# Two batch rows interleaved at the start of an attention and feed-forward kernel, an expansion ahead of the last scores, and the bias on another engine

## The chip, the core and the metric

One core of a Trainium2 chip runs the program. Its engines are TensorE (PE; its weight loads are listed apart as PEld), VectorE (DVE), ScalarE (ACT), GpSimd (POOL) and SyncE (SP, which here only issues transfers). Each engine takes its instructions in a fixed order and waits where one is not ready. The metric is the time of one execution on the device in microseconds (us); less is better.

## What is computed

```python
x = L0_attn_x                                # 8 rows of 512 tokens, 256 wide
x = x + _L0_attn_ref(_layernorm(x), gamma, w_qkv, w_out)
x = x + _L0_ffn_ref(_layernorm(x), router_w, w1, b1, w2, b2)

# attention: 16 heads of 64
xn = rms_norm(x, gamma);  q, k, v = split(xn @ w_qkv)
out = softmax(q * scale @ k.T) @ v;  return out @ w_out
# feed-forward: 8 experts' router, the best two, one shared expert
expert_out = gelu(xt @ w1 + b1) @ w2 + b2
return expert_out * sum(combine)             # sum of the best two's normalized shares
```

The inputs and outputs are float32. `b2` enters each token scaled by that token's share, as all of `expert_out` does.

## The kernel before, in words

**Precision.** Every matmul of size is done in float16 in three parts: a value is split into a high half (rounded) and a low half (what is left), and high x high, low x high and high x low are summed (`PARTS`, L515). So each operand costs a rounding (the "high" function, on ACT or DVE) and a subtraction (the "low" function, on DVE). Weights are scaled by a power of two that is found on the device: sums of squares (`squares`, `square_v`, L206, `square_wo`, L397), a small matmul with ones (`total`, L217), and then nine to twelve tiny DVE instructions (`find_qk`, `find_v`, `find_o`, `find_w`, L265 to L302). After that the weight is split (`split_wv` L383, `split_qk1` L378, `split_wo` L407).

**Attention.** A pair is two heads of one row; a row has 8 pairs, and there are 8 rows. For a pair, `project_qk` (L546) makes Q and K into a ring of two buffers, `scores` (L575) makes four tiles of 128 queries by 512 keys for both heads, of which it returns the row maxima (`top`, DVE), the exponentials (`exp`, ACT, 4 of 128x512 for two tiles), the rounding to `hl` (`high`, ACT) and the low half (`low`, POOL) followed by a transposing transfer into `hT` on SP. `weigh` (L619) multiplies with V six tiles (`LAG`, three steps) later, `divide` (L639) divides by the row sums on DVE, `transpose_o` (L651) turns the result, `project` (L670) applies `w_out` for half of the heads and adds to x. `make_v` (L517) makes V for eight heads of 128 tokens. Row statistics and normalization of the next row are `sums1` (DVE), `scale1`, `scale1_last` and `normalize` (POOL), `transpose_rows` (PE) or, from row 3 on, `split_rows` with a transposing transfer.

**Order.** The order is written out by hand. The main loop (L1072) takes one step `d` per two score tiles, ND = 128 steps. Work beside it is entered with `at(step, pos, fn, ...)` (L853); `pos` says where in the step it runs: "d" after the maxima (one step later than named), "a" matmul groups after the scores, "e" after the exponentials on ACT, "b" after the weighing, "z" at the end.

```python
for d in range(ND + LAG // 2 + 1):
    steps = [scores(n) for n in (2 * d, 2 * d + 1)] if d < ND else []
    for top, _, _, _ in steps: top()
    take_lows(); run(d, "d"); groups = run(d, "a")
    for _, exp, _, _ in steps: exp()
    run(d, "e"); take_highs(groups); take_lows()
    for _, _, high, low in steps: high(); low()
    w = 2 * d - LAG
    if 0 <= w < NS: weigh(w); weigh(w + 1); divide(w // 2)
    take_highs(run(d, "b")); run(d, "z")
```

PSUM holds two score tiles (`ps`), one `po` for the weighing, and a ring of three banks (`bank`, L354) for all other groups, so the group that is third after another waits until that one's result was read.

Before the loop, the first weights are loaded, row 0 is normalized and transposed, and q0, k0 (the weights of heads 0 to 7) are split. In the first steps of the loop come v0 and v1, then q1 and k1 (heads 8 to 15), then `w_out`. Rows are taken one after the other, all 8 pairs of row 0 first. Tuples at L34 say which early roundings are done on DVE.

**Feed-forward.** After the last scores, `expand` (L991) makes h = gelu(y w1 + b1) for one of 8 pieces of 128 columns (6 matmuls, one Gelu on ACT, a rounding on ACT, a low half on DVE), `contract` (L1026) multiplies 8 pieces with w2 for 128 tokens (24 matmuls) and adds bias and x with two DVE instructions and a transfer out. Expansions of a row alternate with contractions of the row before it (L1128). The first six pieces (`EARLY`) of the first row run in the last three steps, between the last weighings.

Of the kernel before, what the change touches and what calls it, by code (L numbers as in the profile page):

```python
# [26 lines left out]
P = 128  # L27
# [4 lines left out]


VECTOR_QK, VECTOR_V, VECTOR_O = (5, 8, 11, 12, 13, 18), (0, 1), (3,)  # L34
CAST_BOTH = (21,)
EARLY = 6
# [46 lines left out]
def preln_block(  # L83
# [71 lines left out]
    for name, off, eng in (  # L155
        ("q0", 0, nc.scalar), ("k0", INNER, nc.sync), ("v0", 2 * INNER, nc.sync),
        ("v1", 2 * INNER + 512, nc.sync),
    ):
        t = staged(f"w_{name}", wqkv_r[:, :, off : off + 512], eng)
        raw[name] = [t[:, c, :] for c in range(NC)]  # L160
    w_r = small.tile([P, NC, NE], F32, name="w_r")
# [35 lines left out]
    def square(name, col, src, scale=1.0):  # L197

        pool, what = (hl_p, "hT") if name in ("qk0", "v", "qk1") else (stage, "stage")
        junk = pool.tile([P, 1024], BF16, tag=what, name="junk", bufs=HTB if what == "hT" else SB)  # L200
        nc.scalar.activation(
            junk[:, 0 : src.shape[-1]], src, AF.Square, scale=scale,
            accum_out=sums[name][:, col[0], col[1] : col[1] + 1],
        )

    def square_v(name, col, src, scale=1.0):  # L206
        pool, what, n = (hl_p, "hT", HTB) if name in ("v", "qk1") else (stage, "stage", SB)
        junk = pool.tile([P, 512], BF16, tag=what, name="junk", bufs=n)
        nc.vector.scalar_tensor_tensor(
            junk, src, scale, src, ALU.mult, ALU.mult,  # L210
            accum_out=sums[name][:, col[0], col[1] : col[1] + 1],
        )

    def new_sums(name, k, m):
        sums[name] = stat.tile([P, k, m], F32, name=f"sums_{name}")

    def total(name):  # L217

        _, k, m = sums[name].shape
        pn = bank("pn")  # L220
        nc.tensor.matmul(
            pn[:, 0 : k * m], ones, sums[name].rearrange("p k m -> p (k m)"), start=True, stop=True
        )
        return pn[:, 0 : k * m].rearrange("p (k m) -> p k m", m=m), [
            pn[:, 128 * i : 128 * i + k] for i in range(1, 4)
        ]
# [30 lines left out]
    def with_gamma(*key):  # L257

        f = stat.tile([P, 2, NC], F32, name="f_" + "".join(map(str, key)))
        s = powers_of[key if len(key) > 1 else key[0]]  # L260
        factors[key if len(key) > 1 else key[0]] = f
        for i in range(2):
            nc.scalar.activation(f[:, i, :], gam1, AF.Copy, scale=s[:, i : i + 1])
# [24 lines left out]
    def find_v(n2):  # L288
        added(n2)
        s, u, z = powers("v", n2)  # L290
        powers_of["v"] = s
        factors["1/v"] = inverses("v", u, z)

    def find_o(n2):
        added(n2)
        factors["o"], u, z = powers("o", n2)
        si = inverses("o", u, z)
        f = stat.tile([P, 2], F32, name="f_o")
        nc.vector.tensor_tensor(f, si[:, 0:2], factors["1/v"], ALU.mult)
        factors["1/ov"], factors["1/r"] = f, si[:, 2:3]  # L300
# [21 lines left out]
    with ExitStack() as att:  # L322
# [17 lines left out]
        for b in range(1, XB):  # L340
            load_x(b)
# [3 lines left out]
        xnT, O, OT, po, hT = {}, {}, {}, {}, {}  # L345
        made = {}
# [36 lines left out]
        def split_wv(c, j, eng):  # L383
            if "v" not in factors:
                with_gamma("v")
            cols = ts(j, 512)
            f = factors["v"][:, j, c : c + 1]
# [129 lines left out]
        def make_v(b, t, j):  # L517
# [4 lines left out]
            assert b == 0 or made.get(("pv", b - 1), 0) >= 16 * (j + 1)  # L522
            k = 0
            for i, m in PARTS:
                for c in range(NC):
# [5 lines left out]
            vt = VT[t][:, 8 * j : 8 * j + 8, :]  # L531
# [3 lines left out]
                    nc.vector.tensor_copy if b == 0 and 4 * j + t in VECTOR_V  # L535
# [10 lines left out]
        def project_qk(pair, n):  # L546
# [11 lines left out]
            dst = QK[pair % RING][n]  # L558
            hi, lo = dst[:, 0, :], dst[:, 1, :]

            def high():
                f = factors["out", p // (NP // 2)][:, n : n + 1]
                if 2 * pair + n in VECTOR_QK:
# [11 lines left out]
        def scores(n):  # L575
# [3 lines left out]
            pair, t = divmod(n, NT)  # L579
            need(2, "qk", pair)  # L580
            q, k = QK[pair % RING]
# [19 lines left out]
            def high():  # L601
                if n in CAST_BOTH:
# [16 lines left out]
        def weigh(n):  # L619

            pair, t = divmod(n, NT)
            b, p = divmod(pair, NP)
            need(NT, "v", b, p // 4)
            done("pv", b)
# [3 lines left out]
            for h in range(2):  # L628
                for c in range(NT):
                    v = VT[c][:, 2 * p + h, :]  # L630
# [8 lines left out]
        def divide(k):  # L639
            pair, t = k // 2, k % 2 * 2  # L640
# [10 lines left out]
        def transpose_o(pair):  # L651
# [3 lines left out]
            for t in range(NT):  # L655
# [5 lines left out]
                    nc.vector.tensor_copy if pair in VECTOR_O  # L661
# [138 lines left out]
        for name, k, m in (("qk0", 2, NC), ("v", 2, NC), ("qk1", 2, NC), ("o", 3, 2), ("w", 3, 4)):  # L800
# [10 lines left out]
        for c in range(NC):  # L811
            square_v("v", (0, c), raw["v0"][c], gam2[:, c : c + 1])
# [20 lines left out]
        squares("v", 1, "v1")  # L833
        squares("qk1", 0, "q1", [0])
# [6 lines left out]
        def start_v():  # L841
            find_v(total("v"))
# [53 lines left out]
        at(3, "d", split_wv, 0, 1, nc.scalar)  # L896
        at(2, "d", split_wv, 1, 1, nc.scalar)
        at(4, "e", split_qk1, "q", 0, nc.vector)
        at(4, "e", split_qk1, "q", 1, nc.scalar)
        at(5, "e", split_qk1, "k", 0, nc.vector)  # L900
        at(5, "e", split_qk1, "k", 1, nc.vector)
        at(-1, "d", squares, "qk1", 0, "q1", [1])
        at(0, "z", squares, "qk1", 1, "k1", [0])
        at(2, "b", squares, "qk1", 1, "k1", [1])
        at(3, "b", find_rest, find_qk, 1, "qk1")
        at(2, "d", load_small)
        at(3, "d", load_wo, 0)
        at(5, "d", square_wo, 0, 0)
        at(8, "d", square_wo, 0, 1)
        at(3, "d", load_wo, 1)  # L910
        at(6, "d", square_wo, 1, 0)
        at(6, "d", square_wo_v, 1, 1)
        at(4, "d", square_wr)
        at(10, "b", find, find_o, "o")
        at(12, "d", split_wr)
        at(11, "d", split_wo, 0, nc.scalar)
        at(12, "e", split_wo, 1, nc.scalar)
        at(12, "d", split_wo, 2, nc.scalar)
        at(16, "d", split_wo, 3, nc.scalar)
        for n in (1, 2):  # L920
            for j in range(2):
# [5 lines left out]
                for i in range(2):  # L927
                    at((46, 50, 54, 58, 62, 66, 70, 74)[4 * (n - 1) + 2 * j + i], "z", split_w, n, j, i)
        at(35, "e", square_b1)
        at(44, "b", find, find_w, "w")  # L930
        for b in range(B):
            s0 = 16 * b
            for p in range(NP):
                at(s0 + 2 * p - 2, "a", project_qk, b * NP + p, 0)
                at(s0 + 2 * p - 2, "a", project_qk, b * NP + p, 1)
                if (b, p) != (B - 1, NP - 1):
                    at((s0 + 2 * p + 1 + LAG // 2 + 1) if b else (5, 7, 11, 11, 14, 15, 17, 19)[p], "b", transpose_o, b * NP + p)
            for t in range(NT):
                at(s0 + (13 + 2 * t if b else (13, 15, 17, 19)[t]), "a", project, b, 0, t)
                at(s0 + 3 + 2 * t if b else (5, 8, 4, 10)[t], "a", make_v, b, t, 1)  # L940
                at((s0 - 5 + 2 * t if b > 1 else (11, 13, 13, 17)[t]) if b else (1, 1, 1, 2)[t], "a", make_v, b, t, 0)
            if b + 1 < B:
                at(s0 - 5 if b else 5, "d", scale1_rest, b + 1)
                at(s0 - 4 if b else 5, "d", scale1_last, b + 1)
                for t in range(NT):
                    at(s0 + 21 + 2 * t, "a", project, b, 1, t)
                    at(s0 - 9 + t // 2 if b else (1, 1, 2, 1)[t], "d", sums1, b + 1, t)
                    at(s0 + (1 + t if b else (5, 6, 6, 6)[t]), "d", normalize, norm1, b + 1, t, "x")
                at(s0 - 6 if b else 3, "d", scale1, b + 1)
                if b + XB < B:  # L950
                    for t in range(NT):
                        at(s0 + 30 + 2 * t, "d", load_x_piece, b + XB, t)
                if b + 1 < XD:
                    for c in range(NC):
                        at(s0 + (6 + 2 * c if b else (8, 9)[c]), "b", transpose_rows, b + 1, c)
                else:
                    for k in range(4):
                        at(s0 + (4, 6, 6, 7)[k], "zd"[k // 2], split_rows, "x", b + 1, k)
# [32 lines left out]
        def expand(j, f):  # L991
# [12 lines left out]
            ph = ps_s.tile([P, 2, S], F32, tag="ps", name="ph")[:, 0, :]  # L1004
# [11 lines left out]
            def gelu():  # L1016
# [3 lines left out]
                nc.scalar.activation(hi, h, AF.Copy, scale=factors["h"])  # L1020

            return gelu, lambda: nc.vector.scalar_tensor_tensor(
                lo, h, factors["h"], hi, ALU.mult, ALU.subtract
            )

        def contract(j, t):  # L1026
# [5 lines left out]
            for f in range(NF):  # L1032
# [8 lines left out]
                r, pf[:, :D], factors["1/hw2"], b_2, ALU.mult, ALU.add  # L1041
            )
            nc.vector.scalar_tensor_tensor(
                r, r, comb[:, b, t : t + 1], x2[b][:, t, :], ALU.mult, ALU.add
# [12 lines left out]
        for f in range(EARLY):  # L1057
            at(ND + f // 2, "a", expand, 0, f)
# [13 lines left out]
        for d in range(ND + LAG // 2 + 1):  # L1072
# [10 lines left out]
            take_lows()  # L1083
# [21 lines left out]
        for j in range(1, B):  # L1105
# [7 lines left out]
            if j + 3 < B and order[j + 3] < B - XB:  # L1113
                put(j, 11, load_x2, order[j + 3])
            put(j, 0, both, router_logits, b)
            for k in range(12):
                put(j, min(k + 1, 11), route_step, b, k)
        nc.scalar.activation(first, ones[:, 0:1], AF.Gelu_apprx_tanh)
# [51 lines left out]
```

## Time and profile before

| what | value |
|---|---|
| time, median of 3 runs | 959.67 us (959.57 to 960.41) |
| the profiled execution: time, span | 960.66 us, 958.9 us |
| PE matmul | busy 933.7 us (97%), 11244 matmuls |
| ACT | busy 838.8 us (87%) |
| DVE | busy 733.2 us (76%) |
| POOL | busy 702.6 us (73%) |
| granted TensorE clock, mean | 0.997 |
| start of the first scores, PE | 19.83 us |
| first Gelu, ACT | 774.50 us |
| last matmul group to the end | 954.9 to 958.9 us |

Each engine's timeline gives the start and the length of its instructions and, in brackets, how long the engine was idle ahead of one and what ended that. Instructions of one kind that follow each other stand in one line (x2, x12), whose length is that of the whole group. All instructions of the kernel body carry the line of the helper that issues them (L54); the operation and the tiles tell them apart: `ps` scores, `mx` maxima, `e` exponentials, `hl` the halves of e, `po` weighing, `pot` transposed result, `pqk`, `pv`, `pp`, `ph`, `pf` the groups of Q and K, V, `w_out`, expansion and contraction.

### The profile page before, as it was taken

To read this page: it belongs to the slowest core of one execution; us is meant where nothing else is said; L and a number is where in the kernel's file an instruction comes from. 1 tells how busy PE (TensorE), PEld (TensorE's weight loads), DVE (VectorE), ACT (ScalarE), POOL (GpSimd) and SP (SyncE) were. 2 spreads that over 40 slices of the span, in tenths; PEclk is the share of its full clock that TensorE was granted. 3 is DMA by queue.
4 is the path that set the end of the run, shared out by engine and by line. 5 is a ranking of instruction groups with operands and counts; after the bars stand their busy time and mean duration, and the time that the engine had idled before them with its cause. 6 is when DMAs were issued, how large, how long until landed. Compare 5 with 4: busy or idle time off the path is not lost.

```text
span 958.9 us, 27882 instructions
## 1 busy us (share of the span) xinstructions
PE 933.7 (97%) x11244; PEld 598.5 (62%) x11244; DVE 733.2 (76%) x1325; ACT 838.8 (87%) x1275; POOL 702.6 (73%) x717
## 2 busy tenths in 40 slices
PE   8789999999999999999999999999999999999998
PEld 5345566666666666666666666666666667666666
DVE  6999888888788878788877777777877756655553
ACT  5988899899999999999999999999999986677772
POOL 1688788798888888988888888887888953434400
PEclk9999999999999999999999999999999999999999
DMA  6599899999999999999999999999999971222211
GB/s 220 117 201 191 165 209 204 214 202 198 194 221 202 202 214 209 219 205 207 195 213 184 198 191 185 189 194 193 186 184 197 185 150 34 72 84 77 52 43 39
DMA packets 580624, 163.96 MB, mean 171 GB/s; under 512 B 562960, under 2 KB 578448, under 8 KB 580496
## 3 DMA queue, kind: packets, MB, share of 16 engines
q1 hardware_dynamic: 579952, 161.40, 84.5%
q8 instruction: 88, 1.44, 0.6%
q10 hardware_dynamic: 544, 0.79, 0.2%
q14 instruction: 40, 0.33, 0.1%
HBM read 14.82 MB, written 6.29 MB: 22 GB/s over the span
## 4 chain that ended last, share of the span: by engine, by line
DVE 33%; ACT 27%; PE 26%; issue 7%; POOL 4%; DMA 2%; ACTq 0%; POOLq 0%; DVEq 0%
ACT e L54 19%; DVE mx L54 13%; PE pf L54 9%; PE ph L54 8%; DVE QT L54 4%; DVE O L54 4%; DVE VT L54 4%; DVE KT L54 4%; POOL hl L54 3%; ACT QT L54 3%; PE po L54 2%; ACT VT L54 2%; PE pp L54 2%; PE ps L54 2%; PE pqk L54 2%
## 5 line engine op out<-in xcount | busy, mean ns | idle before, releaser
L54 POOL TENSOR_TENSOR hl<-e,hl 128x512 f16<-128x512 f32 x512 | 585.7, 1176 | 120.4 <-issue 78.5
L54 ACT ACTIVATE e<-ps,mx 128x512 f32<-128x512 f32 x512 | 310.4, 691 | 47.1 <-DVE mx L54 39.1
L54 DVE TENSOR_REDUCE mx<-ps 128x2 f32<-128x1024 f32 x256 | 300.2, 1213 | 1.9 <-PE ps L54 1.9
L54 ACT CAST hl<-e 128x1024 f16<-128x1024 f32 x256 | 258.8, 1081 | 0.0
L54 PEld LDWEIGHTS <-hT 128*128 128x128 f16 x6144 | 203.6, 97 | 33.3 <-issue 5.3
L54 PE MATMUL po<-VT,hT 128*128 128x65 f16 (+1 forms) x6144 | 207.8, 193 | 2.6 <-DVE O L54 1.2
L54 PE MATMUL ps<-KT,QT 64*128 64x512 f16 x1536 | 190.5, 378 | 8.1 <-ACT e L54 6.6
L54 PEld LDWEIGHTS <-wqk 128*128 128x128 f16 x768 | 69.9, 98 | 105.4 <-issue 27.2
L54 PEld LDWEIGHTS <-QT 64*128 64x128 f16 x1536 | 66.3, 94 | 85.0 <-issue 19.8
L54 PE MATMUL pqk<-xT,wqk 128*128 128x512 f16 x480 | 110.7, 380 | 0.4 <-ACT lg L54 0.4
L54 DVE SCALAR_TENSOR_TENSOR QT<-pqk,ab,QT 128x512 f16<-128x512 f32 x64 | 48.0, 750 | 71.8 <-ACT QT L54 71.7
L54 DVE SCALAR_TENSOR_TENSOR h<-h,s_w,h 128x512 f16<-128x512 f32 x64 | 50.0, 783 | 64.8 <-ACT h L54 64.7
L54 PE MATMUL pp<-wo,OT 128*128 128x256 f16 x768 | 94.9, 273 | 0.0
L54 PEld LDWEIGHTS <-OT 128*128 128x128 f16 x768 | 70.2, 98 | 32.6 <-issue 15.3
L54 PE MATMUL ph<-yT,w1s 128*128 128x512 f16 x384 | 89.5, 379 | 0.1
L54 PE MATMUL pf<-w2s,h 128*128 128x256 f16 x768 | 88.4, 273 | 0.0
L54 ACT ACTIVATE h<-ph,b,si_w 128x512 f32<-128x512 f32 x64 | 49.3, 770 | 41.0 <-PE ph L54 40.9
L54 PEld LDWEIGHTS <-h 128*128 128x128 f16 x768 | 75.2, 98 | 14.4
L54 DVE TENSOR_TENSOR VT<-pv,VT 128x512 f16<-128x512 f32 x64 | 43.8, 689 | 50.1 <-ACT VT L54 49.9
L54 PE MATMUL pqk<-xnT,wqk 128*128 128x512 f16 x288 | 66.9, 380 | 1.9 <-DVE OT L54 1.4
L54 PEld LDWEIGHTS <-w1s 128*128 128x128 f16 x384 | 37.0, 98 | 36.8 <-issue 0.3
L54 PE MATMUL pv<-wv,xT 128*128 128x512 f16 x240 | 58.3, 379 | 0.0
(147 smaller groups left out, 929.9 us busy)
## 6 DMA issues: line engine op xcount, KB each, us to landing
hT<-hl SPq DMA_TRANSPOSE x256, 4.0
w<-in_L_ffn_w_dram SPq DMA_DIRECT2D x32, 128.0 KB, 2.8
out_dram<-res SPq DMA_DIRECT2D x32, 128.0 KB, 1.7
x<-x SPq DMA_DIRECT2D x16, 128.0 KB, 2.6
x<-in_L_attn_x_dram SPq DMA_DIRECT2D x16, 128.0 KB, 2.7
x2s<-x SPq DMA_DIRECT2D x4, 512.0 KB, 3.6
x<-in_L_attn_x_dram SPq DMA_DIRECT2D x3, 512.0 KB, 7.5
w_v<-in_L_attn_w_qkv_dram SPq DMA_DIRECT2D x2, 512.0 KB, 8.2
```

Source lines behind the costliest of these rows:

```text
L54: i = method(*args, **kw)
```

## The change

1. **Interleaving.** The order of the work is by groups (row, half of the heads): (0,0), (1,0), (0,1), (1,1), and from row 2 on as before. So q1, k1 and v1 are needed only from group 2 on (step 16; their Q and K are made from step 14, V from step 11), while row 1 must be normalized and transposed by step 3. x of row 1 is loaded ahead of v1. V's buffers are addressed by the parity of the group.
2. **Moves that go with it.** The squares, searches and splits of v1, q1, k1 and w_out stand in other steps and partly on other engines; v0 and v1 get a search each. For row 1 `scale1_last` now stands ahead of `scale1_rest`: the multiplication is done before the reciprocal is taken. Which roundings DVE does is listed by place in the new order.
3. **Last scores.** `EARLY` is 7. The first piece is expanded in step ND-2 into a bank of the ring instead of a score buffer; its Gelu is held until step ND. For the first row the rounding of h moves from ACT to DVE. From step ND on the low halves are no longer taken ahead of the weighing but in the next step.
4. **Bias.** `add_bias` on POOL adds share x b2 to x ahead of the contraction, so that one DVE instruction is left behind each contraction in place of two.

Cut to its core:

```diff
-VECTOR_QK, VECTOR_V, VECTOR_O = (5, 8, 11, 12, 13, 18), (0, 1), (3,)
-CAST_BOTH = (21,)
-EARLY = 6
+EARLY = 7
...
-        ("v1", 2 * INNER + 512, nc.sync),
...
+    load_x(1)
+    t = staged("w_v1", wqkv_r[:, :, 2 * INNER + 512 : 3 * INNER], nc.sync)
...
-    def find_v(n2):
+    def find_v(j, n2):
         added(n2)
-        s, u, z = powers("v", n2)
+        s, u, z = powers(f"v{j}", n2)
...
+        groups = [(0, 0), (1, 0), (0, 1), (1, 1)] + [(b, j) for b in range(2, B) for j in range(2)]
+        turn = {g: u for u, g in enumerate(groups)}
+        seq = [b * NP + j * NP // 2 + p for b, j in groups for p in range(NP // 2)]
...
-        squares("v", 1, "v1")
-        squares("qk1", 0, "q1", [0])
...
-        at(3, "d", split_wv, 0, 1, nc.scalar)
-        at(2, "d", split_wv, 1, 1, nc.scalar)
-        at(4, "e", split_qk1, "q", 0, nc.vector)
-        at(4, "e", split_qk1, "q", 1, nc.scalar)
-        at(5, "e", split_qk1, "k", 0, nc.vector)
-        at(5, "e", split_qk1, "k", 1, nc.vector)
-        at(-1, "d", squares, "qk1", 0, "q1", [1])
-        at(0, "z", squares, "qk1", 1, "k1", [0])
-        at(2, "b", squares, "qk1", 1, "k1", [1])
-        at(3, "b", find_rest, find_qk, 1, "qk1")
+        at(3, "d", square_v, "v1", (0, 0), raw["v1"][0], gam2[:, 0 : 1])
+        at(1, "z", squares, "v1", 0, "v1", [1])
+        at(4, "b", find, find_v, 1, "v1")
+        at(6, "e", split_wv, 0, 1, nc.vector)
+        at(7, "e", split_wv, 1, 1, nc.scalar)
+        at(4, "d", squares, "qk1", 0, "q1", [0])
+        at(5, "z", squares, "qk1", 0, "q1", [1])
+        at(6, "d", square_v, "qk1", (1, 0), raw["k1"][0], gam2[:, 0 : 1])
+        at(7, "d", squares, "qk1", 1, "k1", [1])
+        at(8, "b", find_rest, find_qk, 1, "qk1")
+        at(9, "e", split_qk1, "q", 0, nc.scalar)
+        at(13, "e", split_qk1, "q", 1, nc.scalar)
+        at(10, "e", split_qk1, "k", 0, nc.vector)
+        at(12, "d", split_qk1, "k", 1, nc.scalar)
...
-        at(5, "d", square_wo, 0, 0)
-        at(8, "d", square_wo, 0, 1)
-        at(6, "d", square_wo, 1, 0)
-        at(6, "d", square_wo_v, 1, 1)
+        at(6, "d", square_wo, 0, 0)
+        at(6, "d", square_wo, 0, 1)
+        at(8, "d", square_wo, 1, 0)
+        at(8, "d", square_wo, 1, 1)
...
-        at(11, "d", split_wo, 0, nc.scalar)
+        at(11, "e", split_wo, 0, nc.scalar)
         at(12, "e", split_wo, 1, nc.scalar)
...
+        for i, pair in enumerate(seq):
+            for n in range(2):
+                at(2 * i - 2, "a", project_qk, pair, n)
+            if i + 1 < len(seq):
+                at((5, 7, 9, 11, 13, 15, 17, 19)[i] if i < 8 else 2 * i + 5, "b", transpose_o, pair)
...
+            for t in range(NT):
+                at(s0 - 25 + t // 2 + 3 * (b == 4) if b > 1 else (-1, -1, -1, -1)[t], "d", sums1, b, t)
+            at(s0 - 22 + 3 * (b == 4) if b > 1 else -1, "d", scale1, b)
+            at(s0 - 21 + 3 * (b == 4) if b > 1 else 1, "d", scale1_rest, b)
+            at(s0 - 20 + 3 * (b == 4) if b > 1 else 0, "d", scale1_last, b)
+            for t in range(NT):
+                at(s0 - 15 + t if b > 1 else (1, 1, 1, 1)[t], "d", normalize, norm1, b, t, "x")
+                at(s0 - 10 + 2 * c if b > 1 else (2, 3)[c], "b", transpose_rows, b, c)
...
-            ph = ps_s.tile([P, 2, S], F32, tag="ps", name="ph")[:, 0, :]
+            ph = bank("ph") if ahead else ps_s.tile([P, 2, S], F32, tag="ps", name="ph")[:, 0, :]
...
-                nc.scalar.activation(hi, h, AF.Copy, scale=factors["h"])
+                if j:
+                    nc.scalar.activation(hi, h, AF.Copy, scale=factors["h"])
+            def low():
+                if j == 0:
+                    nc.vector.tensor_scalar(hi, h, factors["h"], None, ALU.mult)
+                nc.vector.scalar_tensor_tensor(lo, h, factors["h"], hi, ALU.mult, ALU.subtract)
...
+        def add_bias(b, t):
+            g, c = nc.gpsimd, comb[:, b, t : t + 1]
+            if t == 0:
+                f = tiny.tile([P, NT], F32, tag="shares", name="shares")
+                g.tensor_scalar(f, comb[:, b, :], factors["1/hw2"], None, ALU.mult)
...
+            g.tensor_scalar(bias, b_2, c, None, ALU.mult)
+            g.tensor_tensor(x2[b][:, t, :], x2[b][:, t, :], bias, ALU.add)
...
-                r, pf[:, :D], factors["1/hw2"], b_2, ALU.mult, ALU.add
-            )
-            nc.vector.scalar_tensor_tensor(
-                r, r, comb[:, b, t : t + 1], x2[b][:, t, :], ALU.mult, ALU.add
+                r, pf[:, :D], shares.pop((b, t)), x2[b][:, t, :], ALU.mult, ALU.add
...
-        for f in range(EARLY):
-            at(ND + f // 2, "a", expand, 0, f)
+        held = []
+        at(ND - 2, "a", lambda: held.append(expand(0, 0, True)))
+        at(ND, "a", held.pop)
+        for f in range(1, EARLY):
+            at(ND + (f - 1) // 2, "a", expand, 0, f)
...
-            take_lows()
+            if d < ND:
+                take_lows()
...
+            for t in range(NT):
+                put(j, 3 * t, add_bias, order[j - 1], t)
...
+        for t in range(NT):
+            put(B - 1, 11, add_bias, order[B - 1], t)
```

## The prediction

> **What bounds the kernel now.** I read the stretches first, then the waits of TensorE (PE), then the timelines of VectorE (DVE) and ScalarE (ACT). The table of stretches has, after the length, busy us of PE, weight load, DVE, ACT, GpSimd (POOL), then granted clock, DMA share, GB/s:
>
> ```profile
> 20.00:40.00 20.00, 17.11 (x98) 6.92 (x94) 19.26 (x41) 19.77 (x39) 8.92 (x8) 1.00 0.32 66
> 40.00:60.00 20.00, 15.33 (x210) 9.09 (x208) 19.45 (x40) 17.87 (x32) 17.86 (x19) 1.00 0.99 212
> 60.00:80.00 20.00, 17.37 (x224) 9.98 (x220) 19.52 (x35) 19.06 (x32) 17.45 (x18) 1.00 0.79 178
> 80.00:105.00 25.00, 22.64 (x298) 13.28 (x295) 24.45 (x45) 22.22 (x37) 21.68 (x24) 1.00 1.02 170
> 105.00:130.00 25.00, 25.00 (x322) 15.88 (x321) 21.61 (x34) 22.54 (x35) 19.14 (x18) 1.00 0.87 199
> 755.00:795.00 40.00, 37.41 (x512) 25.57 (x509) 26.26 (x50) 34.05 (x53) 24.96 (x26) 1.00 0.81 154
> 795.00:945.00 150.00, 150.00 (x1134) 103.69 (x1133) 86.03 (x232) 106.72 (x149) 51.56 (x81) 1.00 0.22 60
> ```
>
> From 105 us PE is never idle for long: its matmuls set the time, and the change leaves their number as it is. PE is idle 25.2 us of 958.9 (span less 933.7 busy). About 17.5 lie before 102 us, where DVE is full; about 2.6 lie in 755:795; about 4 at the end. Only these can move. In 20:105 DVE is busy 82.7 of 85 us, so **DVE sets the pace of the start**.
>
> Call a step the two score tiles that one turn of the main loop computes, S(n) the start of step n's score matmuls and M(n) the start of its row maxima on DVE. From the timelines: S(5) 53.82, S(15) 116.08, S(17) 126.52; M(0) 21.50, M(3) 41.78, M(5) 56.01, M(13) 105.62. How one step is chained on DVE, from the steady stretch:
>
> ```profile
> 111.61 2.35 DVE L54 TENSOR_REDUCE mx<-ps 128x2 f32<-128x1024 f32 x2
> 115.95 0.75 DVE L54 SCALAR_TENSOR_TENSOR QT<-pqk,ab,QT 128x512 f16<-128x512 f32 x1 [1.99 <-ACT QT L54]
> 116.62 0.74 DVE L54 SCALAR_TENSOR_TENSOR KT<-pqk,ab,KT 128x512 f16<-128x512 f32 x1
> 117.28 0.17 DVE L54 RECIPROCAL rden<-po 128x4 f32<-128x4 f32 x1
> 117.48 0.42 DVE L54 TENSOR_TENSOR O<-po,rden 128x256 f32<-128x256 f32 x1
> 117.83 2.34 DVE L54 TENSOR_REDUCE mx<-ps 128x2 f32<-128x1024 f32 x2
> ```
>
> The maxima release ACT's four exponentials, ACT then rounds QT (the high half), DVE waits 1.99 us for that, forms the two low halves, divides, and only then takes the next maxima: 6.2 us. Constants from these timelines: exponentials begin M+1.31 and last 2.29; an ACT copy out of PSUM 0.48, a QT or KT rounding 0.57, a weight split 0.62, a 128x512 square 0.72, the two casts to hl 1.89; on DVE a low half 0.60 to 0.66, a low half of a weight 0.68 alone and up to 1.5 beside POOL, divide 0.54, search for a power of two 1.7 to 2.4, statistics 0.53 per tile. The next scores start at M+2.63 at the earliest (M 56.01, 62.77, 68.34 and 79.83; S 58.64, 65.39, 70.97 and 82.46).
>
> **The start: interleaving.** From S(0) to M(13) DVE has, by these rows, 82.7 us of work in the old order; the profile took 84.1. Adding up the changed order the same way gives 82.3. The splits of the second halves (q1, k1, v1) move from steps 3 to 5 to steps 6 to 13, but row 1's statistics come forward into step 0, the v search is made twice (+1.7), and squares of v1 and k1 move to DVE (+1.4) while one square of w_o (1.4), a split leave it. So DVE's sum is no smaller; **what counts is whether its queue stays full.** I walked the two in-order queues step by step:
>
> - Step 0 carries 11.1 us of DVE instead of 8.6 (four statistics 2.1, one more rounding 0.66): M(1) 32.6 (was 30.12), M(2) 37.3 (35.37).
> - Step 2: POOL's scale chain for row 1 stands ahead of the first hl. It waits for the statistics (29.2), takes 3.1 to 3.9, then 4 hl (4.5), 4 more for step 1, then four normalizations of 0.55: 43.8 to 44.6. PE's transposes of row 1 wait for that and for the bank that QT's low half frees (41.8, then two 1.3 us groups). S(3) 44.0 to 44.8, M(3) 45.2 (41.78).
> - Steps 3 and 4 are light now: 3.6 and 7.2 us against 4.3 and 9.9. M(5) 56.0: level with 56.01.
> - Steps 5 to 8: ACT receives q1's square, two of w_o (1.44), k1's square, two more of w_o. Step 6 costs ACT 7.0, so the exponentials of step 7 start 0.7 late; there wv's low half waits on DVE for its ACT split (exponentials + 2.29 + 0.62): 1.8 us idle. In step 8 QT's low half waits 0.2 to 1.5. M(9) 81.2.
> - Step 9: the qk1 search and half the statistics of row 2, 7.7. Step 10: 6.15. Step 11: the o search and a w_o low half, 7.45. M(12) 102.5.
> - Steps 12 and 13: the ACT splits now stand behind the exponentials, and the low half that DVE has next waits 1.2 in each: 7.5 and 6.1. M(14) 116.1, S(15) 118.7.
>
> Against S(15) 116.08 that is 2.6 later, and 2.5 us less matmul work has been issued by then (91.0 against 93.5 by row durations; the two are level at S(17)). **Start: +5.0 us.** From there PE has enough to do. Bounds: with no DVE wait at all M(13) is 21.5 + 82.3 + the old order's excess of 1.4 = 105.2, and S(17) 126.0: -0.5. Upward, the ten weight low halves and squares on DVE in steps 4 to 13 cost up to 0.7 more each than I took beside POOL, some on the path: +6.5. I take 5.0, because the chain printed above is the nearest row and every even step from 6 to 14 has it.
>
> The Trainium skill (SBUF — State Buffer, Who interferes with whom) says that a DVE instruction with two SBUF inputs contends with a GpSimd instruction that reads SBUF, each blocking the other for its whole length. The trace agrees in size: a w_o low half took 0.75 at 108.29 and 1.49 at 130.33. It speaks against the bias on POOL beside 64 low halves of h; by the rule up to 64 x 0.56 = 36 us of DVE delay (estimate), by the rows none.
>
> **The last scores.** TensorE's timeline:
>
> ```profile
> 761.87 0.82 PE L54 MATMUL ps<-KT,QT 64*128 64x512 f16 x6 [0.33 <-ACT e L54]
> 762.62 1.63 PE L54 MATMUL po<-VT,hT 128*128 128x65 f16 x48
> 765.52 0.82 PE L54 MATMUL ps<-KT,QT 64*128 64x512 f16 x6 [1.27 <-ACT e L54]
> 788.49 0.44 PE L54 MATMUL pot<-ident,O 128*128 128x128 f32 x2 [0.37 <-DVE O L54]
> ```
>
> The last scores wait 1.27 us for ACT. The early piece is six matmuls (1.30) put just ahead of that po group: the hole fills, the scores start when they did, and one piece less follows. -1.3. Its bank is freed by the held Gelu two steps later; the third allocation after it comes in step ND+1, behind that Gelu, so nothing waits. The low halves of h move behind the divide: in the old order DVE's divides at 778.16 and 787.80 stood behind low halves, and PE lost 0.28, 0.25 and 0.37. -0.9. The roundings of eight h pieces move from ACT (0.63) to DVE (0.47 to 0.67, from the split rows): 5 us on a DVE that is idle 13.7 of 40; nothing. Bounds: -1.2 to -2.4.
>
> **The bias.** Each of 32 contractions loses one 0.48 us DVE instruction and gains two on POOL: tensor_scalar 128x256 0.56 to 0.6, and a tensor_tensor 128x256, not in the trace, between 0.56 and the 1.18 of 128x512; I take 0.6. POOL goes from 52 to about 90 us busy in 795:945. A bias is queued one expansion and one contraction (3.9) before it is needed and PE has three banks, so 4 to 8 us of lateness cost nothing. Queued behind it on POOL are the router and normalization steps of the next rows, whose uses lie a row (21 us) ahead. The last row's biases can start at 945.3 (last router sum), 1.2 each, done by 950.5, before the last contraction ends. There the path loses one instruction:
>
> ```profile
> 954.88 0.48 DVE L54 SCALAR_TENSOR_TENSOR res<-pf,f_w,b 128x256 f32<-128x256 f32 x1 [1.61 <-PE pf L54]
> 955.40 0.48 DVE L54 SCALAR_TENSOR_TENSOR res<-res,comb,x2s 128x256 f32<-128x256 f32 x1
> ```
>
> -0.5 (954.88 to 955.40). The upper end, if biases are late, is rival D.
>
> **Sum:** +5.0 - 1.3 - 0.9 - 0.5 = +2.3. The profiled execution had a span of 958.9 and took 960.66, 0.1% above the median of 959.67; its span becomes 961.2, its time about 963.0, the median **962.0**.
>
> **Rivals.**
> A (forecast): DVE's queue runs dry behind ACT, 962.0, one and a half either way. Chance 0.50.
> B, the other side: DVE's queue stays full, since the work is the same and the old order showed hardly a wait in 20:105. Start -0.5, total -0.5 - 2.2 - 0.5 = -3.2: 956.5. It decides if DVE waits less than about 1 us for ACT and PE between M(0) and M(13). Against it: row 1's transposes hang on POOL, and the splits stand behind the exponentials. Chance 0.20.
> C: half the waits are there; start +2.5, total -0.2: 959.5. For it: ACT has 5 to 6 us per step against a DVE of 6, so an ACT lag of 0.7 may vanish. Chance 0.22.
> D: as A, and POOL is late with biases: its router steps wait up to 8.2 us for DVE in this trace, and a bias behind one stalls PE once its banks are used up; 0.5 us in each of seven rows, +3.5: 965.5. Against it: the slack above. Chance 0.08.
>
> **Numbers.** Two tenths of a per cent, 1.9 us, is about what a measurement here tells from no change. Slower by more: 0.36 of A's 0.50 and D, 0.44. Faster: 0.18 of B. Within: 0.14 of A, 0.02 of B, C: 0.38. The range 957.0 to 964.2 leaves out about half of B, D, and A's edge. A alone: 960.5 to 963.5.
>
> **What would show it.** In the changed profile: S(3), behind row 1's first transposes, near 44.5; M(5) near 56; DVE idle behind ACT of 1 us or more in steps 7, 12 and 13; S(17) near 131.5 (126.0 says B). No wait before the last scores. One res instruction per contraction, the end 0.5 closer to the last matmul. PE without gaps from 135 to 755 and in the expansions; gaps there behind res would say D. If DVE is full to M(13) and S(17) is still late, my PE count is wrong.

## The result, and the profile after

| | us, median | runs | ratio to before, 95% interval |
|---|---|---|---|
| before | 959.62 | 959.51 to 960.41 | |
| the change | 963.74 | 963.07 to 964.25 | 1.0045 [1.0033, 1.0057] |

Slower by 4.1 us. The profiled execution took 963.07 us with a span of 961.3. Against the profile of before that is only +2.4, because that execution of before started late: its M(0) is at 21.50 us, where the change has 19.53 and the twelve kernels below 19.83 to 20.31. So everything in the start is counted from M(0) below. In every kernel with the interleaving, row 1 is scaled by 1/(norm x rstd) where before has rstd/norm (the multiplication stands ahead of the reciprocal; rstd is one over the standard deviation). The two agree only where rstd is 1, so for row 1 these kernels leave out the right scale. No instruction is added or left out by that; an interleaving with the right scale was not timed.

The table of stretches of the changed kernel (length, busy us of PE, weight load, DVE, ACT, POOL, granted clock, DMA share, GB/s):

```profile
20.00:40.00 20.00, 14.76 (x68) 5.51 (x67) 19.55 (x41) 14.43 (x23) 12.34 (x15) 0.91 0.29 60
40.00:60.00 20.00, 19.05 (x237) 10.83 (x235) 17.12 (x33) 17.71 (x27) 16.92 (x18) 1.00 1.00 180
60.00:80.00 20.00, 17.46 (x222) 10.12 (x221) 17.16 (x33) 19.51 (x38) 13.52 (x13) 1.00 1.13 225
80.00:105.00 25.00, 20.46 (x279) 12.38 (x279) 22.98 (x55) 21.70 (x37) 19.86 (x21) 1.00 0.67 143
105.00:130.00 25.00, 22.26 (x280) 13.71 (x277) 21.40 (x32) 23.27 (x37) 19.61 (x19) 1.00 0.89 181
755.00:795.00 40.00, 38.24 (x516) 25.59 (x513) 31.29 (x60) 31.57 (x48) 29.82 (x33) 1.00 0.94 172
795.00:945.00 150.00, 150.00 (x1141) 103.14 (x1139) 76.86 (x201) 107.17 (x151) 97.29 (x142) 1.00 0.22 60
```

DVE, full before (82.7 of 85 us in 20:105), is busy 76.8 of 85 now, and PE, which had no gap in 105:130, loses 2.7 us there. The expansions are still without gaps. DVE's timeline shows for whom it waits, in the brackets:

```profile
43.63 2.36 DVE L50 TENSOR_REDUCE mx<-ps 128x2 f32<-128x1024 f32 x2 [1.17 <-PE ps L50]
...
71.87 0.75 DVE L50 SCALAR_TENSOR_TENSOR wv<-w_v,f_v,wv 128x512 f16<-128x512 f32 x1 [1.30 <-ACT wv L50]
...
105.42 1.33 DVE L50 SCALAR_TENSOR_TENSOR wo<-w_o,s_o,wo 128x512 f16<-128x512 f32 x1 [1.35 <-ACT wo L50]
...
112.90 0.75 DVE L50 SCALAR_TENSOR_TENSOR wqk<-w_q,f_qk,wqk 128x512 f16<-128x512 f32 x1 [1.37 <-ACT wqk L50]
...
130.69 0.75 DVE L50 SCALAR_TENSOR_TENSOR wo<-w_o,s_o,wo 128x512 f16<-128x512 f32 x1 [1.43 <-ACT wo L50]
```

The first is step 3 behind row 1's transposes, the others are low halves of weights whose high half ACT makes behind the exponentials. PE at the last scores, and DVE at the end:

```profile
770.08 0.82 PE L50 MATMUL ps<-KT,QT 64*128 64x512 f16 x6
...
793.32 1.47 PE L50 MATMUL ph<-yT,w1s 128*128 128x512 f16 x6 [0.96 <-DMA yT<-yhl]
```

```profile
958.00 0.48 DVE L50 SCALAR_TENSOR_TENSOR res<-pf,shares,x2s 128x256 f32<-128x256 f32 x1 [2.14 <-PE pf L50]
```

The wait of 1.27 us ahead of the last scores is gone, the waits for divides are gone too, and one res instruction is left; new is a wait of 0.96 us for a transposed y.

### The profile page after: what moved, and what is told of

Same layout as the page of the kernel before. It is cut to its first block, busy times and chain, and to the rows that moved or that the text cites. A ratio compares the mean times of both kernels' runs of the same rounds, so it can differ in the third digit from the quotient of the medians.

```text
span 961.3 us, 27960 instructions
## 1 busy us (share of the span) xinstructions
PE 935.3 (97%) x11246; PEld 597.9 (62%) x11246; DVE 724.1 (75%) x1311; ACT 834.2 (87%) x1266; POOL 755.2 (79%) x789
## 4 chain that ended last, share of the span: by engine, by line
PE 35%; DVE 23%; ACT 22%; issue 6%; POOL 5%; DMA 2%; ACTq 0%; POOLq 0%; DVEq 0%
ACT e L50 16%; DVE mx L50 10%; PE pf L50 9%; PE ph L50 8%; PE po L50 5%; PE ps L50 4%; PE pqk L50 4%; POOL hl L50 4%; DVE O L50 3%; DVE QT L50 3%; PE pp L50 3%; DVE VT L50 3%; DVE KT L50 3%; ACT QT L50 3%; PE pv L50 2%
## 5 line engine op out<-in xcount | busy, mean ns | idle before, releaser
L50 ACT CAST hl<-e 128x1024 f16<-128x1024 f32 (+1 forms) x256 | 258.7, 1080 | 0.0
L50 DVE SCALAR_TENSOR_TENSOR h<-h,s_w,h 128x512 f16<-128x512 f32 x64 | 52.5, 821 | 60.3 <-ACT h L50 60.0
```

The costliest lines, as they stand in the source:

```text
L50: i = method(*args, **kw)
```

## The experiments

Ratios are to the kernel before, measured on the same chip.

**1. The parts one by one.** `tail_only` is before with this core of part 3 (and EARLY 7), `bias_only` before with part 4, `tail_bias` both, `inter_only` the changed kernel without both.

```diff
+        at(ND - 2, "a", lambda: held.append(expand(0, 0, True)))
+        at(ND, "a", held.pop)
...
+                if j:
                     nc.scalar.activation(hi, h, AF.Copy, scale=factors["h"])
+            def low():
+                if j == 0:
+                    nc.vector.tensor_scalar(hi, h, factors["h"], None, ALU.mult)
...
+            if d < ND:
                 take_lows()
```

> The kernel before with part 3 of the change alone (piece ahead of the last scores, eight roundings of h on DVE, low halves behind the weighing). Theory: the stretch 755 to 795 loses 1.27 us ahead of the last scores and 0.9 us of divide waits, and gains up to 0.96 us where the first contraction or expansion waits for POOL's y: -1.2 to -2.2 us against before, the first contraction 1.5 to 2.2 earlier counted from the first scores of step 100. Rival: the roundings on DVE keep POOL's route waiting, and what is won is given back behind it: 0 within 0.5.

> The kernel before with part 4 alone (bias added on POOL). Theory: only the last group loses one DVE instruction: -0.5 us; no PE wait for a bank or for res in 795 to 945. Rival: POOL, some 45 us busier there, delays a router or normalization step, or DVE's low halves beside it grow: +0.5 to +3.5.

> The kernel before with parts 3 and 4, so the change without the interleaving. Theory: the sum of the two, -1.7 to -2.7 us against before, about 957.3, and the change minus this is the price of the interleaving, +6 to +7. Rival: the parts at the end cost time themselves and the interleaving only little: at or above before.

> The changed kernel with parts 3 and 4 undone, so interleaving alone. Theory: DVE runs dry behind ACT in the first 17 steps and row 1's first normalization holds step 3: +5 to +6.5 us against before, 965 to 966; the wait ahead of the last scores is back. Rival: the start is worth nothing to either side (within 1 us) and the changed kernel's loss is made at the end.

| kernel | us | ratio | step 126's scores to first contraction |
|---|---|---|---|
| before | 960.03 | | 35.18 us (760.71 to 795.89) |
| tail_only | 957.43 | 0.9974 [0.9964, 0.9984] | 33.81 (759.90 to 793.71) |
| bias_only | 959.54 | 0.9996 [0.9987, 1.0005] | 35.20 (760.04 to 795.24) |
| tail_bias | 957.35 | 0.9972 [0.9962, 0.9982] | 32.70 (760.28 to 792.98) |
| inter_only | 966.37 | 1.0065 [1.0053, 1.0078] | |

The last column is read from one trace of each kernel, the times are medians. -2.7 for parts 3 and 4 together and +6.3 for the interleaving make +3.6, against +4.1 measured. So the whole loss is the interleaving; the rest of the change is a gain, and **tail_bias is faster than both kernels**. Part 4 alone can't be told from no change; its trace has the last res instruction 0.5 us closer, and no PE wait behind it.

**2. Is it the wait for ACT?** `lows_later` takes the waiting low halves of weights only after the next maxima; with `defer` for the second of v1 and of q1 and three of w_out; `row1_late` moves row 1's normalization and, with it, two V tiles; `both_late` is both.

```diff
-            part_qk(n, 1, c, eng=eng)()
+            low = part_qk(n, 1, c, eng=eng)
+            later_lows.append(low) if defer else low()
...
+        at(5, "d", with_gamma, "v1")
-        at(7, "e", split_wv, 1, 1, nc.scalar)
+        at(7, "e", split_wv, 1, 1, nc.scalar, True)
...
             run(d, "z")
+            lows.extend(later_lows)
+            later_lows.clear()
```

```diff
-                at(s0 - 15 + t if b > 1 else (1, 1, 1, 1)[t], "d", normalize, norm1, b, t, "x")
+                at(s0 - 15 + t if b > 1 else (2, 2, 2, 2)[t], "d", normalize, norm1, b, t, "x")
-                    at(s0 - 10 + 2 * c if b > 1 else (2, 3)[c], "b", transpose_rows, b, c)
+                    at(s0 - 10 + 2 * c if b > 1 else (3, 4)[c], "b", transpose_rows, b, c)
-                    at(((1, 1, 2, 2), (4, 5, 7, 9))[u][t], "a", make_v, b, t, j)
+                    at(((1, 1, 2, 2), (5, 6, 7, 9))[u][t], "a", make_v, b, t, j)
```

> The changed kernel; the low halves of five weight tiles that ACT splits behind the exponentials (v1, q1, three of w_out) are taken on DVE only after the maxima of the next step, and the factor of v1 is made one step earlier. Same instructions, another order. Theory (the loss is DVE's queue that waits for ACT): five waits of 1.00, 1.30, 1.35, 1.37 and 1.43 us go, 6.4 in all, and some come back as waits for the exponentials: -3 to -5 us against the changed kernel, 959 to 961. Rival (the waits only fill time that the chain maxima, exponentials, rounding needs anyway): the wait moves to QT's or VT's low half, 0 to -1.

> The changed kernel; row 1's four normalizations on POOL and its two groups of transposes stand one step later, and its second V tile at step 6 instead of 5. Theory: the scores of step 3 no longer stand behind POOL's row 1 chain; M(3) comes near 41.5 instead of 43.6; -1 to -2.5 us against the changed kernel if DVE, light in steps 3 and 4, has the later work ready. Rival: the same work lands in steps 4 to 6, M(6) and the total stay: 0 within 0.7.

> The two edits before this together. Theory: they act at different places and add: -4 to -7 us against the changed kernel, M(0) to M(17) near 108 instead of 113.7, no DVE wait over 1 us left between steps 4 and 17. Rival: DVE's sum of work sets the time whatever the order; less than 2 us.

969.32 (1.0099 [1.0084, 1.0114]), 973.73 (1.0143 [1.0129, 1.0157]) and 979.62 (1.0206 [1.0192, 1.0220]): all slower than the change, which neither side expected. Two lines of DVE's timeline and one of PE's waits (waited for: us in total, times, longest) of `lows_later`:

```profile
72.79 0.69 DVE L50 TENSOR_TENSOR VT<-pv,VT 128x512 f16<-128x512 f32 x1 [1.67 <-ACT VT L50]
...
77.14 1.74 DVE L50 SCALAR_TENSOR_TENSOR wv<-w_v,f_v,wv 128x512 f16<-128x512 f32 x1
```

```profile
PE pqk L50 <- DVE wqk L50: 4.1, 1, 4.1
```

Up to M(14) four waits with 5.0 us are out of their places, and M(14) is 94.97 us after M(0) instead of 95.19: nothing gained. In step 7 DVE now waits 1.67 us for V's copy, which also stands behind the exponentials, and the low half that was taken out takes 1.74 us in the next step, beside POOL, instead of 0.75. The loss behind that is the edit's own: q1's low half, now after the maxima of step 14, holds that step's Q and K on PE for 4.1 us. In `row1_late` it is POOL's order, in POOL's and PE's timelines:

```profile
43.47 4.50 POOL L50 TENSOR_TENSOR hl<-e,hl 128x512 f16<-128x512 f32 x4 [2.45 <-ACT hl L50]
47.96 2.18 POOL L50 TENSOR_SCALAR x<-x,nm,norm 128x256 f32<-128x256 f32 x4
```

```profile
48.57 2.10 PE L50 MATMUL pt<-ident,x 128*128 128x128 f32 x4 [3.78 <-POOL x L50]
```

M(3) does come 1.2 us earlier (22.86 after M(0), from 24.10), but the normalization now stands behind four more hl, which wait for step 3's exponentials: PE's transposes start at 48.6 instead of near 41. DVE then waits 6.12 us for step 4's scores, and one of PE's V groups waits 3.31 us (64.54) for the second transposed half, which also comes a step later. The loss grows: M(13) is 98.63 us after M(0), from 89.00.

**3. The same, without a later step.** After that my theory was that the chain maxima, exponentials, ACT's result, low half sets a step. `splits_ahead` puts ACT's splits ahead of the exponentials of the same step, `v_even` V's tiles into the even steps; `ahead_even` is both.

```diff
-        at(7, "e", split_wv, 1, 1, nc.scalar)
+        at(5, "d", with_gamma, "v1")
+        at(7, "e", split_wv, 1, 1, nc.vector)
-        at(13, "e", split_qk1, "q", 1, nc.scalar)
+        at(12, "d", split_qk1, "q", 1, nc.scalar)
-        at(12, "e", split_wo, 1, nc.scalar)
+        at(11, "d", split_wo, 1, nc.scalar)
-        at(16, "e", split_wo, 3, nc.scalar)
+        at(15, "d", split_wo, 3, nc.scalar)
```

```diff
-                    at(((1, 1, 2, 2), (4, 5, 7, 9))[u][t], "a", make_v, b, t, j)
+                    at(((1, 1, 2, 2), (4, 6, 8, 10))[u][t], "a", make_v, b, t, j)
+                elif u == 2:
+                    at(12 + 2 * t, "a", make_v, b, t, j)
```

> The changed kernel; three splits that ACT does behind the exponentials (the second of q1, the second and the fourth of w_out) stand ahead of them in the same step, the second of v1 goes to DVE, and v1's factor is made a step earlier; no DVE instruction is put into a later step. Theory now: a step lasts as long as the chain maxima, exponentials, ACT's split or rounding, DVE's low halves behind it, so splits that leave this chain shorten steps 6, 7, 12, 13 and 16 by 0.6, 0.7, 1.2, 0.9 and 0.3: -2 to -4 us against the changed kernel, 960 to 962. Rival: as where the low halves came later, the wait turns up at the next low half that hangs on the exponentials: 0 to -0.5.

> The changed kernel; the V tiles of the second and third group stand in the even steps (6, 8, 10 and 12, 14, 16, 18), where Q and K make DVE wait for ACT anyway, instead of the odd ones. Theory: odd steps 5 to 15 lose a DVE instruction that hangs on the exponentials and some 0.5 to 1 us each, even ones gain 0.6: 0 to -2 us against the changed kernel, and S(17) as much earlier. Rival: the ring of three banks (Q, K, V and a transpose in one step) makes PE wait, +1 to +3.

> The two edits together. Theory: in odd steps 7, 13 and 15 nothing on DVE hangs on the exponentials any more, so these come near the 4.2 to 4.5 us of the old order's short steps: -4 to -6 us against the changed kernel, 958 to 960. Rival: the sum of DVE's work, which is the same in both orders, sets the time: M(0) to M(17) stays above 111, under 2.5 us gained.

963.63 (1.0038 [1.0026, 1.0051]), 966.47 (1.0066 [1.0052, 1.0080]) and 965.24 (1.0053 [1.0041, 1.0066]), against 963.74 of the change. `splits_ahead` is no faster than the noise allows to tell, although its waits are nearly gone; in its trace S(17) lies 110.46 us behind M(0), 0.8 us earlier than in the change. DVE's waits from 54 to 128 us, 6.4 us in the changed kernel, are these:

```profile
DVE VT L50 <- ACT VT L50: 0.4, 1, 0.4
DVE QT L50 <- ACT QT L50: 0.3, 1, 0.3
DVE wo L50 <- ACT wo L50: 0.2, 1, 0.2
```

What took their place stands in the lengths. DVE's timeline, and POOL's:

```profile
104.74 1.73 DVE L50 SCALAR_TENSOR_TENSOR wo<-w_o,s_o,wo 128x512 f16<-128x512 f32 x1
...
110.58 1.13 DVE L50 SCALAR_TENSOR_TENSOR wqk<-w_q,f_qk,wqk 128x512 f16<-128x512 f32 x1
111.64 1.64 DVE L50 SCALAR_TENSOR_TENSOR wqk<-w_k,f_qk,wqk 128x512 f16<-128x512 f32 x1
```

```profile
105.88 1.61 POOL L50 TENSOR_TENSOR hl<-e,hl 128x512 f16<-128x512 f32 x1
107.78 4.95 POOL L50 TENSOR_TENSOR hl<-e,hl 128x512 f16<-128x512 f32 x4 [0.29 <-ACT hl L50]
```

The same three instructions took 1.33, 0.75 and 0.74 us in the changed kernel, where the first two came later in their step and the third came ahead of the second. In their new places they meet POOL's low halves (hl), of which four take 4.50 undisturbed, 1.13 each. The longer square of k1 (0.80 to 1.26), a cast of hl (0.42 to 0.96), a small split of the router's weights (wr, 0.23 to 1.03) and a rounding of v1 (0.49 to 0.93) belong to it. Another 1.36 is work that came over from ACT, the second rounding of v1, which takes 0.47 to 0.49 at its shortest. From M(0) to M(16), with the waits added up from the brackets of DVE's timeline and the rest taken as busy:

| | M(0) to M(16) | waits | busy |
|---|---|---|---|
| tail_bias (old order) | 100.24 | 3.01 | 97.23 |
| the change | 106.79 | 8.79 | 98.00 |
| splits_ahead | 106.14 | 3.32 | 102.82 |

5.5 us of waits left and 4.8 us of busy time came: by the lengths of the instructions 1.4 for the rounding from ACT, the rest for instructions that grew longer. The Trainium skill (SBUF — State Buffer, Who interferes with whom) says that a DVE instruction with two SBUF inputs and a POOL instruction that reads SBUF exclude each other, the one that is issued first holding the other. The lengths agree, 1.73 for 0.74 at its shortest and POOL's hl 1.61 for 1.13, and so does a case of the other order: in the changed kernel the low half at 110.79 took 0.74 beside four hl, and those took 5.00 instead of 4.50. (The same section says that casts and scalings can, under conditions, use both port pairs and then contend with POOL too; 0.42 to 0.96 for the cast fits that.) So part of the waiting cost nothing: while DVE waited for ACT, POOL had the way free. How much of the waiting that was, no run shows, since this edit also gave DVE more to do.

`v_even` fails by its rival, the ring of three banks; PE's timeline:

```profile
77.69 1.47 PE L50 MATMUL pv<-wv,xnT 128*128 128x512 f16 x6 [1.62 <-DVE OT L50]
...
91.55 2.74 PE L50 MATMUL pv<-wv,xnT 128*128 128x512 f16 x6 [2.49 <-DVE OT L50]
```

Five such waits take 7.5 us: Q, K, V and a turned result in one step are four groups on three banks. `ahead_even` has the same groups in one step: M(0) to M(17) is 114.42 us, above 111, as its rival had it.

**4. The end.** `piece_only` is before with the early piece alone (the first two lines of the first diff, and EARLY 7); `tail_bias_y` is `tail_bias` with the last two router steps of the first row one step later.

```diff
-            at(ND - 6 + (0, 1, 2, 3, 4, 4, 5, 6, 6, 6, 7, 8)[k], "d", route_step, r0, k)
+            at(ND - 6 + (0, 1, 2, 3, 4, 4, 5, 6, 6, 6, 8, 8)[k], "d", route_step, r0, k)
```

> The kernel before with only the one expansion piece ahead of the last scores (EARLY 7); roundings of h stay on ACT, low halves where they were. Theory: -1.3 of the -2.6 us measured for the whole of part 3 is this piece, the rest the divides and a smaller queue of ACT: 958.7 against 960.0. Rival: the piece alone brings it all, -2 or more, or its Gelu's bank makes PE wait and it brings nothing.

> The kernel before with parts 3 and 4, and the last two router steps of the first row one step later, so that POOL forms the low halves of the next row's y ahead of its wait of 3.8 us for DVE. Theory: the wait of the expansion for the transposed y (1.1 us in one profile, absent in another) cannot come any more: 0 to -1 us against the same kernel without the edit, about 956.5 to 957.3. Rival: that transfer is set by its own length, 0 within 0.3.

`piece_only` is slower than before: 961.21 against 960.06, 1.0013 [1.0004, 1.0021]. PE's timeline:

```profile
776.11 2.88 PE L54 MATMUL ph<-yT,w1s 128*128 128x512 f16 x12 [0.55 <-ACT h L54]
779.72 1.61 PE L54 MATMUL po<-VT,hT 128*128 128x65 f16 x48 [0.73 <-DVE O L54]
...
790.70 0.44 PE L54 MATMUL pot<-ident,O 128*128 128x128 f32 x2 [1.79 <-DVE O L54]
```

The hole ahead of the last scores is filled (-1.27), but ACT has a Gelu and a rounding more in the same steps, DVE's low halves wait 8.4 us for its roundings in 755:800 (7.1 before), and the divides stand behind them: 0.55 + 0.73 + (1.79 - 0.37) = 2.7 comes back. The stretch to the first contraction is 36.52 us, 1.34 longer. `tail_bias_y` is at 957.44 (0.9973 [0.9962, 0.9984]): no gain. The wait for y is not there, but `tail_bias` happened to have none in its profile either, while `tail_only` had 1.10; a wait of 0.5 us of PE for OT stands in its place. The traces show what decides: of the nine kernels here that have part 3 with this router order, the change among them, six have the wait (0.96 to 1.1), and in these the transposing transfer of y lands 5.2 to 5.4 us after its issue; in the other three (`tail_bias`, `v_even`, `ahead_even`) it lands after 3.6 to 3.8, and nothing waits. What makes it take longer is not shown.

## Why the prediction was right, and where it was not

- **Sign and forecast case:** A, slower, 963.74 inside 957.0 to 964.2, 1.7 above the forecast and 0.2 above case A's own 960.5 to 963.5.
- **DVE's sum of 82.3 us from S(0) to M(13):** right. From M(0) it is 89.00 less 6.48 of waits, 82.5.
- **The walk through the queues:** right in its places. Counted from M(0), forecast and measured: M(1) 11.1 and 11.05, M(2) 15.8 and 15.70, S(3) 22.5 to 23.3 and 23.24, M(5) 34.5 and 35.16, M(9) 59.7 and 60.70, M(12) 81.0 and 81.51, M(14) 94.6 and 95.19. The waits of steps 7, 8, 12 and 13 were 1.30, 0.30, 1.35 and 1.37. The waits of 0.91 in step 2 (V's copy) and of 1.00 in step 6 (v1's factor, from ACT) it did not have.
- **Start +5.0:** too small. S(17) lies 111.24 us behind M(0), before 105.02: +6.2, and the interleaving alone costs +6.3. The forecast for S(17) from M(0) was 110.0; half of the miss was there by M(5) and S(15), at 97.8 against 97.2. The other half lies between S(15) and S(17), 13.4 us where the forecast has 12.8: a score tile waits 0.33 us there for the exponentials (118.50), and from then on PE has no wait up to S(17). The wait of 1.43 us in step 16, which the forecast did not count, makes M(17) late, but holds no matmul.
- **"What counts is whether its queue stays full":** not enough as a reason. In `splits_ahead` DVE waits as little as in the old order (3.3 us up to M(16)) and the start is only 0.8 us shorter than in the change. The waits are where the time shows; in the one edit that took them away, the instructions beside POOL grew longer and a rounding came to DVE. My upper bound had this price ("up to 0.7 more each ... beside POOL"), my sum did not.
- **Last scores -1.3 and -0.9:** nearly right together, -1.5 in the trace of the change and -2.5 in that of `tail_bias`, which lacks the wait of 0.96 for y; wrong as two terms. The piece alone costs 1.2 us: it pays only together with the roundings that leave ACT and the low halves that leave the divides' way. Which of these two it needs was not separated. "Nothing" for the roundings on DVE was wrong: with them POOL's router step waits 3.83 us for DVE (785.42; 2.25 before), the low halves of y start 1.3 us later (20.3 us behind step 126's first scores, 19.0 before), and where the transfer behind them is slow as well, one expansion waits 0.96.
- **Bias -0.5:** right in the trace (958.00 is the last, one instead of two); POOL is busy 97.3 us in 795:945 instead of 90, the tensor_scalar takes 0.94 and the tensor_tensor 0.78 to 0.81 on average where I took 0.56 and 0.6. DVE's low halves of h beside it take 0.81 us on average in `bias_only`, 0.75 before: some 3.4 us over the 55 of 795:945, neither the estimate of 36 nor none, and PE has no gap there. Rival D did not come: the last group waits for PE.
- **Readings:** PE's idle time before 102 us is 16.5, not about 17.5; the 84.1 and 82.3 us of DVE run from M(0), not from S(0); a low half of a weight takes at least 0.72, not 0.68. None of these moves the sum by more than about 0.5.
- With the measured terms the sum is +6.2 - 1.5 - 0.5 = +4.2, against +4.1 of the medians.

What stays open: the old order runs M(0) to M(16) with 97.2 us of DVE and hardly a wait; in the interleaved order I found either 98.0 with 8.8 of waits or 102.8 with 3.3. How much of that is work that the order adds (the second search for v, two squares), how much the rounding moved to DVE and how much the meeting with POOL was not separated by a run, and an interleaving that loses nothing was not found.

## What to carry to other kernels

A wait in an in-order queue is not always a price that is won back by filling it: ask first what the neighbour does in that time, and what the same instruction takes beside it. An edit that fills a hole of the bound engine can be worth nothing while the engine behind it (here ACT, whose roundings hold DVE's low halves and with them the divides) has not been relieved in the same stretch; cost such edits together, not as terms of a sum. When parts of a change lie in different stages, run each alone: here two parts won 2.7 us and one lost 6.3.

## What the runs showed of the hardware

- A 128x512 low half of a weight takes 0.72 us on DVE at its shortest (85.97 in the change) and up to 1.74 (`lows_later`) beside POOL's 128x512 tensor_tensor, which itself goes from 1.13 to as much as 1.70 (`both_late`). POOL's 128x256 tensor_scalar took 0.55 on average in the normalizations and, for the bias, 0.94 in the expansions.
- The granted clock fell to 0.91 in 20:40 us of the change and to 0.83 in `inter_only`, where PE was idle 5.2 and 4.4 us of 20; before it was idle 4.7 us in 40:60 at a clock of 1.00. The difference between the two cost nothing: M(0) to M(17) is 113.69 and 113.74 us.
- The start varies from trace to trace, without an edit ahead of it: M(0) of the kernels with the old order lay at 19.91 to 21.50 us, and it goes with the first loads. The 512 KB of w_q landed after 5.9 us in `tail_only` (M(0) 19.91), 6.3 in `tail_bias` (20.31) and 7.4 in before (21.50).
- A transposing transfer of y landed 3.6 to 3.9 us after its issue in some traces and 5.2 to 5.4 in others.
